# A two-pass filter and mixture-of-experts kernel: vector work of the setup put into waits, the first tiles worked off in the setup, and transposes three tiles ahead in the second pass

## The chip, the cores and the metric

The kernel runs on one core of one Trainium2 chip. The metric is the time of one execution on the device, in microseconds (us). Inside the core five engines work side by side, each through its own instructions in order: TensorE (PE: matrix multiplications and transposes), VectorE (DVE), ScalarE (ACT), GpSimd (POOL: here mostly indirect gathers and scatters) and SyncE (SP: it only issues transfers). They meet at semaphores.

## The reference, cut to what matters

The input is x of 16 x 1024 tokens with 512 features each. N is the number of tokens, 16384.

```python
xn = layernorm(x)                                  # per token
# branch s: a filter over the features, and a correction by 24 bits
D    = fractal_dimension(xn)                       # one number, from the first 1024 values of xn
x1   = ifft(fft(xn) * wave_filter(D, 512)).real    # a fixed linear map, given D
bits = (x1 @ W_el + b_el > 0)                      # 24 bits a token
c    = golay_correct(bits)                         # 12 syndromes; up to 3 bits are flipped
s    = x1 + c @ W_le + b_le
# branch g: two of eight experts for each token
p        = softmax(xn @ router_w.T)
w, e     = top2(p);  w = w / (sum(w) + 1e-6)
g        = silu(sum over the two of (xn @ expert_weights[e] + p[e]) * w)
out  = x + s * g
```

Whatever route a token takes, it is multiplied by two 512 x 512 expert matrices in float32.

## The kernel before, in words

**Two passes over 128 tiles of 128 tokens.** The first pass (`pass_1`, L1053) reads x in blocks of four tiles. For each tile g it sums the halves of a row and gets its total (`total`, L422, on DVE), sums the squares (`spread`, L447, on ACT), forms sums and differences for the filter (`fold`, L484: two instructions `sd` on DVE, one `mm` on POOL), transposes the four quarters on PE and copies them to SBUF on ACT (`transpose`, L498), multiplies them with the filter's matrices `cs`, `cd`, `cm` on PE and scales the outcome into `yb` on ACT (`filt`, L512). `scale` (L456) turns the sums of squares of a group of eight tiles into 1/deviation, in three steps on ACT and DVE; `level` (L441) writes the means of four tiles on ACT. Every four tiles `store` (L530) writes `yb` to a DRAM buffer `yd`. Behind this, for groups of 8 and of 16 tiles, run the correction of the bits (`code`, L553) and the routing (`route`, L615), which sorts the tokens by pair of experts into `lists` with indirect scatters (L771).

**The setup** (`setup`, L250, after `loads`, `constants` and `more_constants`) comes ahead of the first pass. A chain that no engine can leave computes D: DVE sums pieces of x, PE adds them over partitions (L267), DVE counts (L272 to L278), PE adds again (L279), ACT takes a logarithm (L282), DVE forms an angle, ACT a sine (L296), DVE scales the bases (L307), PE multiplies them (L311, L316), and ACT and PE complete `cs`, `cd`, `cm` (L325 to L352). After that come `total` and `spread` of the first eight tiles. Tile 0 alone is folded and transposed in the setup.

**Order.** The order on each engine is the order in which the program is written (`tc.manual_schedule()`); nothing reorders it. In pass 1, step g of the loop issues `fold(g + 2)`, a few `total` and `spread` for tiles up to `AHEAD_S` = 11 ahead, `transpose(g + 1)`, two operations of `setup_code` (constants for later, on DVE) and `filt(g)`; then come one scatter and one piece each of the waiting lists `now`, `routes` and `aside`. An entry `None` in a list ends the step's share: `push` (L1037) runs operations up to the next `None`.

```python
            while spreads and spreads[0] <= g + AHEAD_S and spreads[0] <= 2 * g + GT + 4:
```

**The second pass** (from L1380) runs over 189 tiles sorted by experts: 101 "whole" tiles (all their tokens have the same pair of experts, so two products), 61 "items" (leftover rows for one expert, one product, stored to `ed`) and 27 "rest" tiles (they gather two results of items). 28 whole tiles come first, then the items, then 5 whole, then the rest tiles with the other whole ones among them. Step n issues gathers for tiles ahead (`fetch_tok`, `fetch_x`, `fetch_y` on POOL), `normalize(n + AHEAD_N)` on DVE, and then `work_on(tile n)`:

```python
            pe = product(k, 0)
            scaled(k.acc, pe, k)
            beside()
            added(k, product(k, 1))
```

`product` (L1224) is four float32 matrix multiplications of 128 x 128 by 128 x 512 (L1228). `beside()` issues `turn(n + AHEAD_T)` (L1191: four transposes into the one buffer `pt2`, L1196, and a copy `xt` by ACT, L1198), `turn_code` (L1245: the corrected bits are transposed on PE, L1249, into a PSUM buffer `pc` with one slot and copied by ACT, L1253) and `mend` (L1255: a product with W_le, L1261). In the opening steps two tiles' `turn_code` and `mend` fall into one step, because the records of tile k are taken to be there at step 1 + k // 2 only (`late`, L1365). While the second pass opens, the last routing still drains through `routes`; at its end `whole_ops(1)` (L842) appends its own steps to `aside`. Their first, `lengths` (L849), multiplies the running counts `cum` on PE (L853); DVE has just updated `cum` (L814).

Of the kernel before, what the change touches and what calls it, by code (L numbers as in the profile page):

```python
# [8 lines left out]
F32 = mybir.dt.float32  # L9
# [8 lines left out]
P = 128  # L18
# [15 lines left out]
def kernel(  # L34
# [154 lines left out]
    def constants():  # L189
# [24 lines left out]
        for i, x_ in enumerate(lx):  # L214
            v.memset(st.slope[:, i : i + 1], -(n * x_ - sum(lx)) / den)
        kf = kf[:, 0:KC]
        kr = sp.tile([P, KC], F32, name="kr")
# [11 lines left out]
        v.tensor_scalar(st.by0[:, 1, :], ka, -1.0, -0.5 * math.pi, ALU.mult, ALU.add)  # L229
        v.memset(eps, EPS)  # L230

    def more_constants():
        v, g = nc.vector, nc.gpsimd

        g.iota(tok, pattern=[[BLK, NB], [1, TPT]], base=0, channel_multiplier=TPT)
        g.iota(ti, pattern=[[0, 1]], base=0, channel_multiplier=1)
        g.iota(qi, pattern=[[P, NITEM]], base=0, channel_multiplier=1)
        g.memset(ioff, 0)
        g.memset(ones_b, 1.0)
        g.memset(cum, 0.0)  # L240
        g.memset(ones_f, 1.0)
        for e in range(NE):
            g.memset(iota_e[:, e : e + 1], float(e))
        for r in recs:
            g.memset(r, 0.0)
            g.memset(bits_of(r)[:, :, L : L + 1], 1.0)
        for py in pys:
            v.memset(py[:, 1, X + H : WY], 0.0)

    def setup():  # L250
# [18 lines left out]
        )  # L269
        nc.tensor.matmul(pm[:, NS - 1 :], st.own, sums[:, NS - 1 :], start=True, stop=True)  # L270
        above = sp.tile([P, NS, HW], F32, name="above")
        v.tensor_tensor(  # L272
# [5 lines left out]
        v.tensor_reduce(cnt, above, AX.X, ALU.add)  # L278
        nc.tensor.matmul(pn, st.all, cnt, start=True, stop=True)  # L279
        ly = sp.tile([P, NS], F32, name="ly")  # L280
        v.tensor_scalar(ly, pn, 1.0, None, ALU.max)
        nc.scalar.activation(ly, ly, AF.Ln)  # L282
        nc.scalar.preload_act_table(AF.Sin)
# [17 lines left out]
        v.tensor_add(wp, lat[:, 0:2, :], lat[:, 2:4, :])  # L301
        v.tensor_sub(wt[:, 2:4, :], lat[:, 0:2, :], lat[:, 2:4, :])
        gain = sp.tile([P, KC], F32, name="gain")
        v.tensor_mul(gain, sn[:, 0, :], sn[:, 1, :])
# [9 lines left out]
        for i in range(2):  # L314
            for c in range(2):
                nc.tensor.matmul(  # L316
                    pys[1][:, i, 0:H], bas[:, 2 + c, i * P : (i + 1) * P], gbas[:, 2 + c, :],
                    start=(c == 0), stop=(c == 1),
                )
        v.tensor_add(wt[:, 0, :], wp[:, 0, :], wp[:, 1, :])  # L320
        v.tensor_sub(wt[:, 1, :], wp[:, 0, :], wp[:, 1, :])
        for g in range(2):
            total(g)
            spread(g)
        nc.scalar.copy(cs[:, X:], pys[0][:, 0, 0:Q])  # L325
        nc.scalar.copy(cd[:, X:], pys[0][:, 1, 0:Q])
        for g in range(2, 4):
            total(g)
            spread(g)
        level()  # L330
        nc.scalar.copy(cm[:, :, X:], pys[1][:, :, 0:H])
        v.tensor_scalar(cs[:, L:X], wt[:, 0, L:], 0.25, None, ALU.mult)
        v.tensor_scalar(cd[:, L:X], wt[:, 1, L:], 0.25, None, ALU.mult)
        v.tensor_scalar(cm[:, :, L:X], wt[:, 2:4, L:], 0.5, None, ALU.mult)
        fold(0)
        transpose(0)
# [5 lines left out]
        for i in range(2):  # L342
            for c in range(2):
# [3 lines left out]
                )  # L347
        for op in scale(0, slice(0, TPT)):
            op()
        nc.scalar.copy(cs[:, 0:L], pw[:, 0, :])  # L350
        nc.scalar.copy(cd[:, 0:L], pw[:, 1, :])
        nc.scalar.copy(cm[:, :, 0:L], pw[:, 2:4, :])  # L352
        for g in range(4, GT):
            total(g)
            spread(g)
        level()

# [55 lines left out]
    def bits_of(rec):  # L413
        return rec.bitcast(BF16)[:, :, BITS : BITS + 32]
# [427 lines left out]
    def whole_ops(part: int):  # L842
# [95 lines left out]

        aside.extend([lengths, None, full, None, rows_, None, where, upto, None, bounded])
        aside.extend([experts, None, fetch, None, None, apart, None, turned, None, kept])  # L940
# [112 lines left out]
    def pass_1():  # L1053
# [11 lines left out]
        rest = setup_code()  # L1065
        scales += scale(0, slice(TPT, GT))
        totals, spreads = list(range(GT, NT)), list(range(GT, NT))
        for g in range(-2, NT):
            if (g + AHEAD_L) % TPT == 0 and 4 <= (g + AHEAD_L) // TPT < NB:
                xts[(g + AHEAD_L) // TPT] = load_block((g + AHEAD_L) // TPT)  # L1070
# [5 lines left out]
            if g % TPT == 1 and g > 1:  # L1076
                take_ex(g // TPT - 1)
            if 0 < g + 2 < NT:
                fold(g + 2)
            level()  # L1080
            steps(scales, 1)
            while totals and totals[0] <= g + AHEAD_S + 1 and totals[0] <= 2 * g + GT + 5:
                total(totals.pop(0))
            while spreads and spreads[0] <= g + AHEAD_S and spreads[0] <= 2 * g + GT + 4:
                spread(spreads[0])
                if spreads.pop(0) % GT == GT - 1:
                    scales += scale((g + AHEAD_S) // GT)
            if 0 < g + 1 < NT:
                transpose(g + 1)
            steps(rest, 2)  # L1090
            if g < 0:
                continue
            filt(g)
# [20 lines left out]

    AHEAD_K, AHEAD_X, AHEAD_P, AHEAD_Y, AHEAD_N, AHEAD_T = 9, 6, 4, 5, 4, 2
    BEHIND = 3
# [7 lines left out]

    room = w2.tile([P, 512], F32, name="room", bufs=1)

    class Tile:
# [63 lines left out]
    def turn(k):  # L1191
        if k.kind == "rest":
            return
        pt = ps_x.tile([P, KC * P], F32, name="pt2")
        for c in range(KC):
            nc.tensor.transpose(pt[:, c * P : (c + 1) * P], k.xn[:, c * P : (c + 1) * P], ident)  # L1196
        k.xt = w1.tile([P, KC, P], F32, name="xt2")
        nc.scalar.copy(k.xt.rearrange("p c t -> p (c t)"), pt)  # L1198
# [46 lines left out]
    def turn_code(k):  # L1245
        if k.kind == "item":
            return
        pc = ps_c.tile([96, P], F32, name="pc")
        nc.tensor.matmul(  # L1249
# [89 lines left out]
    for kind in kinds:  # L1339
        tiles.append(Tile(kind, seen.get(kind, 0)))  # L1340
        seen[kind] = tiles[-1].n + 1
    assert seen == {"whole": NPURE, "item": NITEM, "rest": NREST}
    half = NREST // 2
    now += code(NG - 1)
    routes += route(len(rounds) - 1) + [lambda: whole_ops(1)] + [None] * 5
    for op in (rest_b, rest_c, rest_d, rest_e):
# [13 lines left out]
    def each(n, op):  # L1360
# [4 lines left out]
    late = [1 + k // 2 for k in range(NTILE)]  # L1365
    due = {
        "triple": [max(k - 3, late[k]) for k in range(NTILE)],
        "turn_code": [max(k - 2, late[k]) for k in range(NTILE)],
# [5 lines left out]
    def those(n, name, op):  # L1374
        k = range(max(0, n - 2), min(NTILE, n + 5)) if n >= 0 else ()
        for i in k:
            if due[name][i] == n:
                op(tiles[i])

    with tc.manual_schedule():  # L1380
        gone = 0
        for n in range(-AHEAD_K, NTILE + 2):
# [16 lines left out]
            def beside():  # L1399
                each(n + AHEAD_T, turn)  # L1400
                those(n, "turn_code", turn_code)
                those(n, "mend", mend)
# [131 lines left out]
```

## Time and profile before

| what | value |
|---|---|
| median of 3 runs | 1370.36 us (1369.69 to 1370.8) |
| the profiled execution's own time | 1371.99 us |
| its span, first to last instruction | 1370.0 us |
| PE busy | 1323.9 us (97%) |
| DVE busy | 927.1 us (68%) |
| POOL busy | 884.1 us (65%) |
| ACT busy | 602.7 us (44%) |
| mean granted PE clock | 0.990 |
| largest group: expert products, L1228 | 2104 instructions, 940.0 us busy |

The span is the time between the first and the last instruction of one profiled execution; 1.99 us of its own time lie around it. A busy time counts when an engine executed something, and matrix multiplications overlap, so that a busy PE need not be a PE at its peak. "Idle before" an instruction is put down to whatever released it last. The granted clock is the share of full speed that PE was given; where it is 0.5, an instruction of PE takes twice as long.

### The profile page before, as it was taken

The numbers are of one execution on the slowest core, as the hardware profiler recorded it, in microseconds if no ns is written. First come the engines' busy times: TensorE is split into PE (matmuls) and PEld (weight loads), VectorE is DVE, ScalarE is ACT, GpSimd is POOL, SyncE is SP. The second block draws the span as 40 slices with busy tenths as digits, with TensorE's granted clock in tenths as the row PEclk, the third lists the DMA queues.
The fourth block names the chain that finished last, engine by engine and source line by source line (L and its number), as shares of the span: only waits on it lengthen the run. The fifth ranks groups of instructions, "written<-read, shape, count | busy, mean of one in ns | idle before, by whom it ended". The sixth has DMA issues, their size and how long they took to land.

```text
span 1370.0 us, 18162 instructions
## 1 busy us (share of the span) xinstructions
PE 1323.9 (97%) x4944; PEld 737.5 (54%) x4944; DVE 927.1 (68%) x2635; ACT 602.7 (44%) x1298; POOL 884.1 (65%) x879
## 2 busy tenths in 40 slices
PE   5999999989999999999999999999999999999996
PEld 4887777765444444444444444444444444444442
DVE  6898999974765788611111137787778877787775
ACT  6998999975322222222222223333333333333332
POOL 3367777876767554577554046777777777777741
PEclk9999999999999999999999999999999999999998
DMA  6998877836333432355446244555555555655531
GB/s 216 353 319 283 254 243 238 256 108 201 85 104 107 141 109 76 112 170 168 138 141 190 75 134 136 181 173 179 174 172 183 179 176 175 187 173 175 181 121 39
DMA packets 119216, 233.75 MB, mean 171 GB/s; under 512 B 37356, under 2 KB 71020, under 8 KB 115023
## 3 DMA queue, kind: packets, MB, share of 16 engines
q0 software_dynamic: 47264, 135.54, 32.8%
q1 hardware_dynamic: 71386, 96.88, 21.2%
q8 instruction: 43, 0.70, 0.2%
q14 instruction: 55, 0.44, 0.1%
q10 hardware_dynamic: 468, 0.19, 0.1%
HBM read 144.79 MB, written 87.75 MB: 170 GB/s over the span
## 4 chain that ended last, share of the span: by engine, by line
PE 82%; DVE 7%; issue 4%; ACT 2%; POOL 2%; DMA 1%; POOLq 0%; DVEq 0%; SPq 0%; ACTq 0%
PE pe L1228 62%; PE py L521 5%; PE pt L1196 5%; PE pt L502 3%; PE py L518 2%; PE py L519 2%; PE pg L1261 1%; DVE pp L431 1%; DVE sd L490 1%; POOL out L1312 1%; DMA yd<-yb 1%; ACT no L451 1%; DVE sd L493 1%; ACT yb L524 1%; PE pc L1249 1%
## 5 line engine op out<-in xcount | busy, mean ns | idle before, releaser
L1228 PE MATMUL pe<-w_sb,xt 128*128 x2104 | 940.0, 594 | 1.2 <-issue 1.2
L1228 PEld LDWEIGHTS pe<-w_sb,xt 128*128 128x128 f32 x2104 | 394.9, 190 | 417.3 <-issue 411.6
L1279 ACT ACTIVATE acc<-acc,yg 128x512 f32<-128x512 f32 x128 | 92.4, 722 | 406.8 <-DVE acc L1278 406.8
L1278 DVE SCALAR_TENSOR_TENSOR acc<-pe,yg,acc 128x512 f32<-128x512 f32 x101 | 75.7, 749 | 180.2 <-PE pe L1228 180.0
L1198 ACT COPY xt<-pt 128x512 f32<-128x512 f32 x162 | 93.6, 578 | 171.7 <-PE pt L1196 171.7
L1312 POOL DMA_INDIRECT out<-xg,toks x101 | 112.3, 1112 | 82.0 <-DVE xg L1307 55.5
L771 POOL DMA_INDIRECT lists<-rec,dst x128 | 136.6, 1067 | 33.9 <-issue 22.4
L495 POOL TENSOR_TENSOR mm<-xt 128x256 f32<-128x256 f32 x128 | 101.5, 793 | 82.4 <-PE pt L502 63.5
L1189 DVE TENSOR_SCALAR xn<-xg,entry 128x512 f32<-128x512 f32 x61 | 34.8, 571 | 173.4 <-PE pt L1196 170.1
L521 PE MATMUL py<-cm,pmt 128*128 128x288 f32 x512 | 147.2, 411 | 0.0
L1135 POOL DMA_INDIRECT yg<-yd,toks x101 | 107.2, 1061 | 61.6 <-ACT acc L1279 29.6
L1135 POOL DMA_INDIRECT xg<-in_x,toks x101 | 108.6, 1075 | 40.7 <-issue 27.5
L1275 ACT ACTIVATE acc<-pe,yg 128x512 f32<-128x512 f32 x101 | 68.9, 682 | 135.0 <-PE pe L1228 102.4
L1196 PEld LDWEIGHTS pt<-ident,xn 128*128 128x128 f32 x648 | 81.0, 141 | 86.6 <-issue 84.3
L524 ACT ACTIVATE yb<-py,rec 128x640 f32<-128x640 f32 x128 | 101.5, 793 | 26.8 <-PE py L521 23.0
L1135 POOL DMA_INDIRECT xg<-in_x,entry x88 | 89.9, 1021 | 29.6 <-issue 25.9
L1135 POOL DMA_INDIRECT part<-ed,adr_r x54 | 65.7, 1217 | 65.0 <-DMA ed<-res 48.8
L521 PEld LDWEIGHTS py<-cm,pmt 128*128 128x128 f32 x512 | 91.9, 193 | 13.9
L1196 PE MATMUL pt<-ident,xn 128*128 128x128 f32 x648 | 97.3, 273 | 1.6 <-DVE xn L1189 0.8
L1307 DVE TENSOR_TENSOR xg<-mix,xg 128x512 f32<-128x512 f32 x128 | 88.5, 692 | 4.4
L451 ACT ACTIVATE no<-xt,sum 128x512 bf16<-128x512 f32 x128 | 91.0, 711 | 1.2 <-DVE pp L431 1.2
L1135 POOL DMA_INDIRECT entry<-lists,adr_i x61 | 62.9, 1032 | 41.7 <-DVE xn L1189 24.7
(270 smaller groups left out, 1766.1 us busy)
## 6 DMA issues: line engine op xcount, KB each, us to landing
xt<-in_x SPq DMA_DIRECT2D x32, 1024.0 KB
yd<-yb SPq DMA_DIRECT2D x32, 576.0 KB
yd<-yb SPq DMA_DIRECT2D x32, 512.0 KB
ed<-res SPq DMA_DIRECT2D x61, 256.0 KB
w_sb<-in_expert_w SPq DMA_DIRECT2D x8, 1024.0 KB
yd<-rec SPq DMA_DIRECT2D x36, 64.0 KB
lists<-rec,dst POOLq DMA_INDIRECT x128
xg<-in_x,toks POOLq DMA_INDIRECT x101
```

The lines of the kernel that those rows point to most:

```text
L451: nc.scalar.activation(no, xts[g // TPT][:, g % TPT, :], AF.Square, bias=k.sum[:, j : j + 1], scale=-float(E), accum_out=k.sq2[:, j : j + 1],)
L495: nc.gpsimd.tensor_tensor(m, xr[:, 0:H], xr[:, H:E], ALU.subtract)
L521: nc.tensor.matmul(py[:, 1, 0 : X + H], pmt[:, 2 + c, :], cm[:, c, :], start=(c == 0), stop=(c == 1))
L524: nc.scalar.activation(y_room(g), py[:, :, 0:WY], AF.Copy, scale=k.rec[:, j, 11:12])
L771: dma = nc.gpsimd.indirect_dma_start(out=lists, out_offset=bass.IndirectOffsetOnAxis(ap=st.dst[:, j : j + 1], axis=0), in_=st.rec.bitcast( ...
L1135: nc.gpsimd.indirect_dma_start(out=dst, out_offset=None, in_=src, in_offset=bass.IndirectOffsetOnAxis(ap=idx, axis=0), bounds_check=limit - 1,
L1196: nc.tensor.transpose(pt[:, c * P : (c + 1) * P], k.xn[:, c * P : (c + 1) * P], ident)
L1198: nc.scalar.copy(k.xt.rearrange("p c t -> p (c t)"), pt)
L1228: nc.tensor.matmul(pe.unsqueeze(1), k.xt[:, c, :], w_sb[:, bass.ds(e, 1), c, :], start=(c == 0), stop=(c == KC - 1),)
L1279: nc.scalar.activation(k.acc, k.acc, AF.Silu, bias=k.rec[:, 9:10])
L1307: nc.vector.tensor_add(k.x, k.mix, k.x)
L1312: dma = nc.gpsimd.indirect_dma_start(out=of, out_offset=bass.IndirectOffsetOnAxis(ap=k.tok, axis=0), in_=k.x, in_offset=None, bounds_check ...
```

## The change

The change does the following.

- **Setup.** Eight small DVE operations that prepare the angles (`arguments`) move from `constants` to behind the first sums, where DVE has to wait for PE. The clears of the four record buffers move from POOL to DVE (`clear`): one behind the second count, one behind `total(4)`, two into step 4 of the loop. The clears of the two `py` buffers move behind L281. `total(0)` moves ahead of the scaling of the bases. `spread`, `level` and `fold(0)` are spread among the copies of the setup; `fold(1)` and `transpose(1)` are done in the setup; the second half of group 0 is finished in the loop. Totals and spreads run two a step until they are 11 tiles ahead. The steps g = -2 and -1 issue loads only, so that `setup_code` starts two steps later.
- **`whole_ops`.** Its list starts with one more `None`, and six instead of five stand behind the last routing.
- **Second pass.** Addresses, x and the normalized tile are made one step earlier (10, 7, 5 instead of 9, 6, 4), and transposes three tiles ahead instead of two; tiles 0 to 5 keep their two. Step 3 so turns two tiles. `turn` of an item uses the two `pg` buffers when no routing is left. `pc` becomes four slots of one PSUM tile.

```diff
+        v.memset(eps, EPS)
+        st.kf = kf[:, 0:KC]
+
+    def arguments():
+        v, kf = nc.vector, st.kf
         kr = sp.tile([P, KC], F32, name="kr")
...
-        for r in recs:
-            g.memset(r, 0.0)
-            g.memset(bits_of(r)[:, :, L : L + 1], 1.0)
-        for py in pys:
-            v.memset(py[:, 1, X + H : WY], 0.0)
+
+    def clear(r):
+        nc.vector.memset(r, 0.0)
+        nc.vector.memset(bits_of(r)[:, :, L : L + 1], 1.0)
...
         nc.tensor.matmul(pm[:, NS - 1 :], st.own, sums[:, NS - 1 :], start=True, stop=True)
+        arguments()
...
         nc.tensor.matmul(pn, st.all, cnt, start=True, stop=True)
+        clear(recs[0])
         ly = sp.tile([P, NS], F32, name="ly")
         v.tensor_scalar(ly, pn, 1.0, None, ALU.max)
+        for py in pys:
+            v.memset(py[:, 1, X + H : WY], 0.0)
...
         v.tensor_sub(wt[:, 2:4, :], lat[:, 0:2, :], lat[:, 2:4, :])
+        total(0)
...
+        for g in range(1, 4):
+            total(g)
         v.tensor_add(wt[:, 0, :], wp[:, 0, :], wp[:, 1, :])
         v.tensor_sub(wt[:, 1, :], wp[:, 0, :], wp[:, 1, :])
-        for g in range(2):
-            total(g)
-            spread(g)
+        spread(0)
+        level()
+        fold(0)
+        spread(1)
         nc.scalar.copy(cs[:, X:], pys[0][:, 0, 0:Q])
         nc.scalar.copy(cd[:, X:], pys[0][:, 1, 0:Q])
-        for g in range(2, 4):
-            total(g)
-            spread(g)
-        level()
-        nc.scalar.copy(cm[:, :, X:], pys[1][:, :, 0:H])
...
-        fold(0)
+        spread(2)
+        nc.scalar.copy(cm[:, :, X:], pys[1][:, :, 0:H])
         transpose(0)
...
-        for op in scale(0, slice(0, TPT)):
-            op()
+        spread(3)
+        fold(1)
+        begin, middle, end = scale(0, slice(0, TPT))
+        begin()
         nc.scalar.copy(cs[:, 0:L], pw[:, 0, :])
         nc.scalar.copy(cd[:, 0:L], pw[:, 1, :])
         nc.scalar.copy(cm[:, :, 0:L], pw[:, 2:4, :])
-        for g in range(4, GT):
-            total(g)
-            spread(g)
-        level()
+        middle()
+        transpose(1)
+        end()
+        total(4)
+        spread(4)
+        clear(recs[1])
+        total(5)
+        spread(5)
...
-        aside.extend([lengths, None, full, None, rows_, None, where, upto, None, bounded])
+        aside.extend([None, lengths, None, full, None, rows_, None, where, upto, None, bounded])
...
-        scales += scale(0, slice(TPT, GT))
-        totals, spreads = list(range(GT, NT)), list(range(GT, NT))
+        totals, spreads = list(range(6, NT)), list(range(6, NT))
         for g in range(-2, NT):
+            if g == 4:
+                clear(recs[2])
+                clear(recs[3])
...
-            if 0 < g + 2 < NT:
+            if g < 0:
+                continue
+            if g + 2 < NT:
                 fold(g + 2)
...
-            while totals and totals[0] <= g + AHEAD_S + 1 and totals[0] <= 2 * g + GT + 5:
+            while totals and totals[0] <= g + AHEAD_S + 1 and totals[0] <= 2 * g + GT:
                 total(totals.pop(0))
-            while spreads and spreads[0] <= g + AHEAD_S and spreads[0] <= 2 * g + GT + 4:
+            while spreads and spreads[0] <= g + AHEAD_S and spreads[0] <= 2 * g + GT - 1:
...
-    AHEAD_K, AHEAD_X, AHEAD_P, AHEAD_Y, AHEAD_N, AHEAD_T = 9, 6, 4, 5, 4, 2
+    AHEAD_K, AHEAD_X, AHEAD_P, AHEAD_Y, AHEAD_N, AHEAD_T = 10, 7, 4, 5, 5, 3
...
+    pcs = ps_c.tile([96, 4, P], F32, name="pc")
...
-        pt = ps_x.tile([P, KC * P], F32, name="pt2")
+        if k.kind == "item" and not (routes or aside):
+
+            pt = ps_g.tile([P, KC * P], F32, name="pg")
+        else:
+            pt = ps_x.tile([P, KC * P], F32, name="pt2")
...
-        pc = ps_c.tile([96, P], F32, name="pc")
+        pc = pcs[:, k.at % 4, :]
...
-    routes += route(len(rounds) - 1) + [lambda: whole_ops(1)] + [None] * 5
+    routes += route(len(rounds) - 1) + [lambda: whole_ops(1)] + [None] * 6
...
     due = {
+        "turn": [max(k - AHEAD_T, min(k - 2, 3)) for k in range(NTILE)],
...
-                each(n + AHEAD_T, turn)
+                those(n, "turn", turn)
```

## The prediction

> **What bounds the kernel now.** I read four views in this order: the busy times by stretch, what PE waited for, the order of time at the places where it waited, and the granted clock there. The first, with columns start:end, length, busy us of PE, weight loads, DVE, ACT and POOL (with counts), granted clock, DMA share, GB/s:
>
> ```profile
> 0.00:25.00 25.00, 9.51 (x39) 7.97 (x40) 14.94 (x87) 15.06 (x43) 7.04 (x37) 0.91 0.70 255
> 25.00:50.00 25.00, 25.00 (x144) 20.72 (x143) 23.46 (x78) 24.23 (x59) 10.58 (x12) 0.95 0.71 246
> 50.00:75.00 25.00, 24.98 (x166) 20.10 (x166) 21.22 (x80) 24.76 (x63) 8.47 (x12) 1.00 1.01 364
> 75.00:100.00 25.00, 24.99 (x161) 20.26 (x162) 23.21 (x86) 23.78 (x56) 16.01 (x19) 1.00 0.98 306
> ...
> 470.00:800.00 330.00, 330.00 (x1004) 161.93 (x1003) 121.46 (x266) 90.70 (x171) 165.10 (x160) 1.00 0.41 127
> 800.00:1340.00 540.00, 540.00 (x1604) 262.81 (x1603) 418.01 (x1030) 179.41 (x360) 401.61 (x360) 1.00 0.55 170
> ```
>
> From 470 to 1340 us PE has no gap at full clock: a transpose three tiles ahead has nothing to win there. Time can come only from the setup, from pass 1, where ACT is as full as PE, and from PE's few waits (us in total, times, longest):
>
> ```profile
> PE pt L502 <- DVE sd L490: 8.2, 7, 5.2
> PE py L267 <- DVE sums L265: 6.3, 1, 6.3
> ...
> PE pg L853 <- DVE cum L814: 2.6, 1, 2.6
> ...
> PE pc L1249 <- ACT ct L1253: 2.2, 3, 1.0
> ```
>
> The wait of 5.2 us lies ahead of tile 1's transposes, at 23.83. The early loop on ACT, in order of time (start, duration):
>
> ```profile
> 30.36 0.71 ACT L451 ACTIVATE no<-xt,sum 128x512 bf16<-128x512 f32 x1
> ...
> 31.06 0.58 ACT L504 COPY pmt<-pt 128x512 f32<-128x512 f32 x1
> 31.62 0.79 ACT L524 ACTIVATE yb<-py,rec 128x640 f32<-128x640 f32 x1
> 32.31 0.71 ACT L451 ACTIVATE no<-xt,sum 128x512 bf16<-128x512 f32 x1
> ```
>
> One tile is 0.70 + 0.56 + 0.69 = 1.95 us of ACT by starts, with no gap, and PE's tiles are 1.95 us apart too. So a tile started earlier is worth only what ACT's own queue gets ahead.
>
> **Setup: 2.0 us won (0.5 to 4).** Before, DVE reaches L263 at 5.81, though `head` is needed there only and its last packet ended at 2.2. Behind L209 (3.11) stand eight angle operations up to 5.71; they take 0.38 to 0.62 each, and those of their kind at 1.5 to 1.8 took 0.17. They run beside POOL's clears of the records (3.27 to 5.96). With both gone, L263 starts near 3.7, 2.1 earlier. The eight operations now stand behind L265, some 1.3 us unstretched, where DVE waited 1.1 for PE: 0.2 late. The clear of a record (0.51 + 0.17 on POOL, taken for DVE) fits the next wait of 0.68; those of `py`, 0.12, fit the 0.27 behind L281. `total(0)`, 0.42, now waits for block 0 (POOL started on it at 8.35, released by that transfer) and the scaling of the bases waits behind it, another 0.25. With the chain 2.1 - 0.2 = 1.9 early, ACT's last table load ends near 10.4, not 12.2, and the first spread starts there instead of at 12.75: ACT is 2.4 ahead.
>
> From there I count ACT to the start of tile 4's `yb` (35.62 before); the spreads done by then, 0 to 15, are the same 16. ACT's idle time before was 0.69 + 0.48 + 0.19 + 0.74 and some 0.2 of small gaps: 2.3. After: 0.5 until totals 1 to 3 are there (`level` now stands second), 1.1 at the copy of `cm` (PE's L316 runs 3.62 at its cold rate and ends near 14.5), 0.45 ahead of `pmt`, and 0.5 because `total(4)` stands behind `end()` on DVE, which waits for ACT's square, and behind it `total(5)` with a clear between: 2.55. `level` of the second half adds 0.2. 2.4 - 0.25 - 0.2 = 1.95. So `yb` of tile 0 comes near 21.8 instead of 27.7, 6 us earlier, but that of tile 4 only 2 us. The later steps hold the same instructions; the two clears in step 4 (about 1.2 on DVE) and `setup_code` two steps later are covered by ACT, which paces steps 0 to 4 at 2.8 to 3.1 us and the later ones at 1.95 or more. If that cover fails, above all in steps 9 and 10 where L549 and the bits come to DVE too, they cost about 1. The transfers on SP keep their order and move with the tiles.
>
> **The wait for `cum`: 4.1 us won (2.57 to 4.4).**
>
> ```profile
> 381.71 3.60 PE L1228 MATMUL pe<-w_sb,xt 128*128 x8
> ...
> 387.64 0.19 DVE L814 TENSOR_TENSOR cum<-cum,mo 128x28 bf16<-128x28 bf16 x1
> ...
> 387.88 0.23 PE L853 MATMUL pg<-ones_b,cum 128*28 128x128 bf16 x1 [2.57 <-DVE cum L814]
> 388.04 5.40 PE L1228 MATMUL pe<-w_sb,xt 128*128 x8
> ```
>
> L853 stands behind step 5's last product; `cum` is behind `added` of the same step and four routing operations on DVE. One `None` puts L853 behind step 6, by which time `cum` is 5 us old: 2.57 saved. The next product took 5.40 instead of 3.60, and the clock says why:
>
> ```profile
> 385.67:389.09 3.42, 1.21 (x4) 0.67 (x5) 3.35 (x10) 0.72 (x1) 1.69 (x2) 1.00 0.10 15
> 389.09:392.50 3.41, 3.41 (x6) 1.35 (x5) 2.56 (x7) 0.00 (x0) 2.80 (x3) 0.50 0.45 154
> ```
>
> After 3.4 us with 1.21 busy, PE got half its clock for 3.4 us. [...] In this trace windows with 2.46 of 3.4 busy kept the clock and those with 1.64 or less lost it; taking 1.5 idle as the border, a gap of 2.57 at a random phase crosses it in (3.41 + 2.57 - 3.0) / 3.41 = 87%: 2.57 + 0.87 x 1.80 = 4.1. What is late next: step 6's second product needs the buffer that DVE's L1266 and L1267 free (ended 389.1) and would start at 389.5, so 0.4 is left. In pass 1 the same L853 did not wait; its later steps come one later, and `fetch` comes at the same step, for it waits for 16 scatters.
>
> **Turning two tiles in step 3: 2.2 us lost (1.2 to 3.0).**
>
> ```profile
> 363.75 0.58 ACT L1198 COPY xt<-pt 128x512 f32<-128x512 f32 x1
> 364.22 0.27 ACT L1253 CAST ct<-pc 96x128 bf16<-96x128 f32 x1
> 364.54 0.22 PE L1249 MATMUL pc<-ident_b,b 128*96 128x128 bf16 x1 [0.96 <-ACT ct L1253]
> ```
>
> Here tile 6 is turned in the same step as tile 5, with one `pt2`. Its transposes wait for tile 5's copy (to 364.4), end at 364.8; its own copy goes ahead of `ct` on ACT (0.58), so `ct` ends at 365.8, the second `pc` and L1261 follow, and the product, at 364.81 before, starts at 366.1: 1.3. Behind the waiting transposes stand both `pc`, L1261 and tile 3's second product. PE is idle about 1.9 in 2.5 us; by the same border that costs half a clock window in some 52% of phases, 0.9 on average. The four slots of `pc` save nothing: the second L1249 of the changed program is built with a wait for the same count of ACT as before, all four being parts of one PSUM tile. A gain is excluded: nothing is removed there.
>
> **Everything else of the second pass: 0 (-0.5 to +0.5).** The gathers are the same in number, one step earlier; POOL's first `yg` waits 5.2 us for the last store, which covers one gather of 1.0. Item tiles use two buffers where PE never waited for one. Rests of 1.2 to 6 us at POOL and DVE cover `normalize` one step earlier.
>
> **Sum.** 2.0 + 4.1 - 2.2 = 3.9 us. It is made on the profiled execution, 1371.99 us (span 1370.0 and 1.99 around it), which lies 1.63 above the median; a difference carries over: 1370.36 - 3.9 = **1366.5 us**. The bounds of the parts, taken as independent (squares added: 2.0, 0.3, 1.0 and 0.5 upward, 1.5, 1.5, 0.8 and 0.5 downward), give 2.3 to each side: 1364.2 to 1368.8 for this case.
>
> **Rivals.** (1) *The early tiles keep their lead* (8%): if PE and not ACT set the pace of steps 0 to 4, all 6 us stay: 6 + 4.1 - 2.2 = 7.9, 1362.5. For it speaks PE's clock of 0.95 in 25 to 50; against it ACT's 24.23 of 25.
>
> (2) *The setup is swallowed* (18%). From 50 to 100 DMA is busy at 1.01 and 0.98. If its backlog and not the tiles sets the stall that ends with an 11.71 us store at 108.9, nothing of the 2.0 arrives, or half-rate windows in the ramp, where PE has only 1.95 us of work in 3, eat it: 4.1 - 2.2 = 1.9, 1368.5. Against it: DMA is at 0.29 from 24 to 36, so the backlog begins with the tiles.
>
> (3) *The wait moves on* (7%): step 6 then waits for DVE where 0.4 us is left; 2.5 of the 4.1 go: 1.4 won, 1369.0.
>
> (4) *Slower* (7%): ACT's `yb` of tile 36, behind that store, is 2.8 us late today. Were earlier loads to queue ahead of it, a landing of 16 us instead of 11.7 would lose the 3.9; from there on the kernel is slower, at 20 us about 1374. The unchanged order on SP speaks against it.
>
> **How the numbers follow.** The likeliest case has 60%, its own range 1364.2 to 1368.8. A measurement tells 0.2%, 2.7 us, from no change: faster is below 1367.6. Of the 60, 47 lie there and 13 within; rival 1 adds 8 to faster; rival 2 gives 5 to faster and 13 to the same; rival 3 gives 7 to the same; rival 4 gives 7 to slower: 60, 33, 7. The range leaves out rival 4, half of rival 1 and a little of each end: 1361.8 to 1369.6.
>
> **What would show it.** L263 near 3.7 and L267's wait near 4.2, the first `yb` near 22, tile 4's near 33.6, the end of pass 1 (last L521, 326.2 before) 2 us earlier; no wait at the multiplication of `cum` and full clock behind it; a wait of about 1 us at the second transposes of step 3 and no fewer waits at `pc`; from 470 on the same spacing of products. Wrong would make it a stall of another length at tiles 36 to 39, or a half-clock window where I have none.

## The result, and the profile after

The changed kernel took 1363.84 us (median of five runs, 1362.22 to 1366.36), the kernel before beside it 1370.36: a ratio of 0.9955 (95% interval 0.9943 to 0.9966), 6.5 us faster where I had forecast 3.9. The median lies just below the 1364.2 to 1368.8 of the likeliest case and inside the whole range. On the chip of a later comparison it was 1364.16 against 1372.37, 0.9947 (0.9932 to 0.9963). The profiled execution is the one of 1366.36 us, span 1364.3, so the traces show 5.7 us (1370.0 - 1364.3).

The busy times by stretch of the changed kernel, in the columns of the first view shown before:

```profile
0.00:25.00 25.00, 13.38 (x62) 10.87 (x62) 18.19 (x100) 16.41 (x44) 7.28 (x32) 1.00 0.83 297
25.00:50.00 25.00, 24.56 (x135) 19.73 (x136) 22.06 (x77) 24.84 (x63) 8.06 (x10) 0.93 0.70 248
50.00:75.00 25.00, 24.98 (x165) 19.99 (x164) 22.25 (x86) 24.78 (x62) 8.62 (x11) 1.00 0.98 326
...
470.00:800.00 330.00, 330.00 (x1004) 161.90 (x1003) 118.87 (x260) 90.50 (x172) 169.60 (x164) 1.00 0.42 129
800.00:1340.00 540.00, 540.00 (x1597) 262.33 (x1596) 422.64 (x1042) 180.50 (x361) 389.17 (x359) 1.00 0.56 169
```

PE has 13.38 us of work in the first 25, where it had 9.51; from 25 on ACT is full as before (24.84 of 25), and from 470 on nothing has changed. What PE waited for (us in total, times, longest):

```profile
PE py L530 <- ACT pmt L516: 5.5, 3, 3.0
PE py L269 <- DVE kr L222: 3.9, 1, 3.9
...
PE pt L514 <- DVE sd L502: 2.6, 4, 1.0
...
PE pt L1216 <- ACT xt L1218: 1.7, 2, 0.9
...
PE pc L1269 <- ACT ct L1273: 1.3, 2, 0.9
```

The wait of 5.2 for `sd` and the one for `cum` are gone, the first sums are waited for 3.9 instead of 6.3 (the row names `kr`, which ends 0.08 us behind the sums), and a second wait of 0.9 for `xt` is new. The wait for `pmt`, a copy of ScalarE in the first tiles, has grown from 2.4 to 5.5. The setup on ScalarE, the first spread and `yb` of tiles 0 and 4, in order of time (start, duration), before:

```profile
12.75 0.72 ACT L451 ACTIVATE no<-xt,sum 128x512 bf16<-128x512 f32 x1 [0.52 <-DVE pp L431]
...
27.71 0.79 ACT L524 ACTIVATE yb<-py,rec 128x640 f32<-128x640 f32 x1 [0.74 <-PE py L521]
...
35.62 0.80 ACT L524 ACTIVATE yb<-py,rec 128x640 f32<-128x640 f32 x1
```

and in the changed kernel, with ScalarE's longest rest on the way to them:

```profile
9.48 0.72 ACT L463 ACTIVATE no<-xt,sum 128x512 bf16<-128x512 f32 x1
...
11.73 0.21 ACT L456 ACTIVATE low<-sum 128x4 f32<-128x4 f32 x1 [1.44 <-DVE pp L443]
...
21.96 0.77 ACT L536 ACTIVATE yb<-py,rec 128x640 f32<-128x640 f32 x1
...
33.31 0.80 ACT L536 ACTIVATE yb<-py,rec 128x640 f32<-128x640 f32 x1
```

Forecast for the spread and the two `yb` were 10.4, 21.8 and 33.6. And the two places of the second pass, PE in order of time; first step 3 with its two turns, then `cum`:

```profile
360.61 0.60 PE L1216 MATMUL pt<-ident,xn 128*128 128x128 f32 x4
362.07 0.66 PE L1216 MATMUL pt<-ident,xn 128*128 128x128 f32 x4 [0.87 <-ACT xt L1218]
362.57 0.22 PE L1269 MATMUL pc<-ident_b,b 128*96 128x128 bf16 x1
363.56 0.22 PE L1269 MATMUL pc<-ident_b,b 128*96 128x128 bf16 x1 [0.78 <-DVE mix L1292]
...
363.84 3.60 PE L1248 MATMUL pe<-w_sb,xt 128*128 x8
...
387.61 0.60 PE L1216 MATMUL pt<-ident,xn 128*128 128x128 f32 x4
...
391.85 0.23 PE L865 MATMUL pg<-ones_b,cum 128*28 128x128 bf16 x1
392.00 3.70 PE L1248 MATMUL pe<-w_sb,xt 128*128 x8
```

No wait stands ahead of L865, and the product behind it runs at full rate (3.70 where it was 5.40). The row of the second `pc` names `mix` of DVE, which ends at 363.52. The copy `ct`, which that row named before, ends at 363.51, and I read the wait as one for `ct`.

Where the 5.7 us come from, by how much earlier the same instruction starts: the first product of the second pass 3.63 us (326.74 for 330.37); the second `pc` of step 2 only 2.31 (352.42 for 354.73); step 3's product 0.97 (363.84 for 364.81); the transposes of step 6 5.66 (387.61 for 393.27), of which 0.15 goes back when L865 comes. So pass 1 gave 3.6, the first steps of the second pass lost 1.3, the double turn lost 1.3, `cum` gave 4.5: 5.5 of 5.7. The loss of 1.3 was in no step of the prediction.

### The profile page after: what moved, and what is told of

It reads as the page before. It is cut to its first block, busy times and chain, and to the rows that moved or that the text cites. A ratio compares the mean times of both kernels' runs of the same rounds, so it can differ in the third digit from the quotient of the medians.

```text
span 1364.3 us, 18153 instructions
## 1 busy us (share of the span) xinstructions
PE 1324.6 (97%) x4944; PEld 737.2 (54%) x4944; DVE 927.4 (68%) x2643; ACT 602.8 (44%) x1298; POOL 869.5 (64%) x871
## 4 chain that ended last, share of the span: by engine, by line
PE 85%; DVE 4%; issue 4%; ACT 2%; DMA 2%; POOL 1%; POOLq 0%; SPq 0%; DVEq 0%; ACTq 0%
PE pe L1248 62%; PE py L533 7%; PE pt L514 3%; PE pt L1216 3%; PE py L530 2%; PE py L531 2%; PE pg L1216 2%; PE pg L1281 1%; DMA yd<-yb 1%; ACT no L463 1%; POOL out L1332 1%; ACT yb L536 1%; PE pg L581 1%; PE pc L1269 1%; DMA xt<-in_x 0%
## 5 line engine op out<-in xcount | busy, mean ns | idle before, releaser
L533 PE MATMUL py<-cm,pmt 128*128 128x288 f32 x512 | 147.9, 412 | 0.0
L536 ACT ACTIVATE yb<-py,rec 128x640 f32<-128x640 f32 x128 | 101.6, 794 | 25.0 <-PE py L533 20.3
L1151 POOL DMA_INDIRECT part<-ed,adr_r x54 | 62.8, 1164 | 64.9 <-DMA ed<-res 48.7
L1218 ACT COPY xt<-pg 128x512 f32<-128x512 f32 x55 | 32.2, 586 | 153.9 <-PE pg L1216 153.9
L533 PEld LDWEIGHTS py<-cm,pmt 128*128 128x128 f32 x512 | 91.9, 193 | 13.9
L1326 DVE TENSOR_TENSOR mix<-mix,acc 128x512 f32<-128x512 f32 x128 | 87.6, 685 | 0.8 <-ACT acc L1299 0.8
L1216 PEld LDWEIGHTS pt<-ident,xn 128*128 128x128 f32 x428 | 53.4, 141 | 58.4 <-issue 52.2
```

Source lines behind the costliest of these rows:

```text
L533: nc.tensor.matmul(py[:, 1, 0 : X + H], pmt[:, 2 + c, :], cm[:, c, :], start=(c == 0), stop=(c == 1))
L536: nc.scalar.activation(y_room(g), py[:, :, 0:WY], AF.Copy, scale=k.rec[:, j, 11:12])
L1151: nc.gpsimd.indirect_dma_start(out=dst, out_offset=None, in_=src, in_offset=bass.IndirectOffsetOnAxis(ap=idx, axis=0), bounds_check=limit - 1,
L1326: nc.vector.tensor_mul(k.mix, k.mix, k.acc)
```

## The experiments

The kernel before took 1372 us in the runs of front_only, two_buffers, warm_entry and after_again; that chip and the one of the result are called the quiet ones here. It took 1447 and 1460 us in the two other groups. On those chips every kernel stands still for long in the second pass (the one before by its time, the others in their traces), as in this wait of PE in the page of no_ahead:

```profile
PE pc L1264 <- ACT ct L1268: 23.9, 3, 21.6
```

The copy that PE waits for there stands on ScalarE behind rests that the profile puts down to nothing it shows. Pass 1 runs as on the quiet chips up to tile 120. Its last seven tiles already take 17.1 to 17.8 us there, not 14.6, and from the last group of pass 1 to the first product of the second pass it is 7.2 to 8.3 us, not 5.0 to 5.3. The steps between the stalls have their usual lengths again. So from those groups I read positions up to tile 120 and durations; their ratios have wide intervals and decide nothing about a few us.

**cum_only, cum_only_2: the step of `cum` alone.**

```
-        aside.extend([lengths, None, full, None, rows_, None, where, upto, None, bounded])
+        aside.extend([None, lengths, None, full, None, rows_, None, where, upto, None, bounded])
-    routes += route(len(rounds) - 1) + [lambda: whole_ops(1)] + [None] * 5
+    routes += route(len(rounds) - 1) + [lambda: whole_ops(1)] + [None] * 6
```

> The kernel before with one step more ahead of the counting matmul of `cum`, and nothing else. The prediction's row says 2.57 us of wait and 1.80 us of half clock behind it go, weighed 4.1: some 1366.3 us, no gap ahead of that matmul, the granted clock 1.00 behind it. [...] A third reading comes from the trace of the changed kernel, whose pass 1 gains another 1.3 us between tiles 112 and 120, where the same edit shifts the first part's counting by a step: then 5.5 us go, 1364.9, and pass 1 of this kernel ends 1.3 us earlier than before.

> The same kernel as cum_only, on another chip, since the first one stalled some tens of us in the second pass. By the traces so far 2.73 us of idle and counting and 1.80 us of half clock go and 0.16 of the counting comes back a step later: 4.4 us, a ratio to the kernel before of 0.9968. If only the wait counts (2.57): 0.9981. The end of pass 1 is that of the kernel before, within the 1.7 us of one half-clock window.

Measured 0.9927 (0.989 to 0.9965) and 0.9933 (0.9908 to 0.9958), both among stalls. PE has no wait at the counting in either trace, and the product behind it takes 3.70. Pass 1 gains nothing: `yb` of tile 120 starts at 311.62 and 311.91, before 311.67. The reading that counts a gain in pass 1 is refuted. Both intervals lie below the 0.9968 of the row: some 10 us went where 4.4 were expected. A step more may move the stalls too; that was not tested, and these ratios don't size the term. On the quiet chips the edit was not run alone, but from step 3's product to the end of the span it is 1005.2 us in both traces with the wait (before, front_only) and 1000.5 to 1000.9 in the four without it: 4.3 to 4.8.

**setup_only, setup_only_2: the setup alone**, the second pass and `cum` as before.

> The kernel before with the setup and the first steps of the changed one, its second pass and the step of `cum` unchanged. The prediction says 2.0 us are won (0.5 to 4): 1368.4 us, with `yb` of tile 4 and of tile 112 both some 2 us early. If the 3.6 us by which pass 1 of the changed kernel ended earlier in its trace all belong to the setup, 1366.8. If the early lead is swallowed before the end of pass 1, 1370.4.

> The same kernel as setup_only, on another chip. By the prediction 2.0 us, a ratio of 0.9985. By the positions in the traces since (2.7 us at tile 8, another 0.75 between tiles 40 and 104) 3.4 us, 0.9975. The constants alone were measured at 0.9985 (0.9977 to 0.9994); if the new order of the first tiles adds nothing, this run agrees with that.

Measured 0.9985 (0.9951 to 1.002) and 0.9985 (0.9961 to 1.0008): undecided. In the traces `yb` of tile 4 starts at 32.23 and 33.05 (35.62 before) and that of tile 120 at 308.17 and 307.39 (311.67 before): the 3.6 us by which pass 1 of the changed kernel ends earlier come with the setup alone. Both still hold the wait for `cum`, in other executions and on other chips. PE in setup_only:

```profile
405.64 3.60 PE L1243 MATMUL pe<-w_sb,xt 128*128 x8
411.80 0.23 PE L865 MATMUL pg<-ones_b,cum 128*28 128x128 bf16 x1 [2.56 <-DVE cum L826]
```

and two clock windows of setup_only_2 (the first view's columns; PE busy, and the granted clock after POOL):

```profile
409.80:413.22 3.42, 0.99 (x3) 0.58 (x4) 3.35 (x9) 0.72 (x1) 2.81 (x3) 1.00 0.49 151
413.22:416.63 3.41, 3.41 (x5) 1.35 (x4) 2.74 (x7) 0.00 (x0) 2.50 (x4) 0.50 0.07 18
```

In all four traces that have the wait with PE idle in it (before, setup_only, setup_only_2, front_only) it is 2.56 or 2.57 and the product behind takes 5.40. The half clock follows a window with 0.99 us of 3.42 busy here, 1.21 in the trace of before, and it belongs to the price.

**warm_gap: the wait kept, PE busy in it.**

```
+            if part:
+                for _ in range(5):
+                    nc.tensor.matmul(pg, ident, w_sb[:, 0, 0, :], start=True, stop=True)
             nc.tensor.matmul(k.pc, cum, ones_b, start=True, stop=True)
```

> The kernel before with five more matmuls of 128x512 (about 2.1 us of PE) into the same PSUM tile just ahead of the second part's counting matmul of `cum`, which overwrites them: the wait for `cum` stays as long, but PE is not idle in it. If a window with about a third of busy PE brings half clock, the product behind the wait takes 3.6 us instead of 5.4 and the kernel is 1.8 us faster, 1368.6 us. [...]

```profile
402.54 4.45 PE L856 MATMUL pg<-w_sb,ident 128*128 128x512 f32 x10
406.92 0.23 PE L857 MATMUL pg<-ones_b,cum 128*28 128x128 bf16 x1
407.08 3.70 PE L1232 MATMUL pe<-w_sb,xt 128*128 x8
```

The product behind takes 3.70 and not 5.40: with PE busy in the wait, no half clock followed in this trace. But the five run in ten passes of 0.43, twice what I had counted, and last 4.4 us where the wait plus the lost clock was 4.4: mechanism shown, time none (0.996, 0.9918 to 1.0002).

**front_only: the constants of the setup alone.** The order of totals, spreads, folds and transposes stays.

```
-        for r in recs:
-            g.memset(r, 0.0)
...
+        arguments()
         above = sp.tile([P, NS, HW], F32, name="above")
...
+        clear(recs[0])
         ly = sp.tile([P, NS], F32, name="ly")
```

> The kernel before with only the constants part: the angle arguments behind the first sums, the clears of the records and of `py` on VectorE in its waits; the order of totals, spreads, folds and transposes is untouched. The prediction puts the win of the setup into this front chain (1.9 us early, 2.4 on ScalarE) and counts the new order of tiles as nothing or 0.2 lost: then the first spread starts near 10 us, `yb` of tile 8 comes 2 to 2.7 us before the 43.9 of the kernel before, as in the run with the whole setup (41.4 on average of three), and pass 1 ends as early as there. The rival: the tiles folded and turned in the setup bring it; then `yb` of tile 8 here stays within 1 us of 43.9.

Measured 0.9985 (0.9977 to 0.9994), 1370.45 against 1372.37 us. ScalarE, the first spread and `yb` of tile 8:

```profile
10.85 0.72 ACT L458 ACTIVATE no<-xt,sum 128x512 bf16<-128x512 f32 x1 [1.38 <-DVE pp L438]
...
41.63 0.80 ACT L531 ACTIVATE yb<-py,rec 128x640 f32<-128x640 f32 x1
```

Start of `yb` in the traces, us (old setup: before, cum_only, cum_only_2, warm_gap; new: the nine others without front_only):

| tile | old setup | constants alone | new setup |
|---|---|---|---|
| 0 | 27.1 to 27.8 | 25.42 | 20.8 to 22.4 |
| 8 | 43.3 to 44.9, mean 44.2 | 41.63 | 40.4 to 42.1, mean 41.4 |
| 120 | 310.8 to 311.9, mean 311.5 | 308.26 | 304.6 to 310.2, mean 307.2 |

The first spread starts at 10.85, not near 10: it waits 1.38 for its total. On the means the new order is 3.8 us ahead of the constants alone at tile 0, and at tile 8 some 0.2. Up to there the constants carry the gain, the tiles folded and turned early hardly any, and the rival expectation falls; but the constants alone have one trace, and at tile 8 the nine others differ by 1.7.

Behind tile 8 this does not hold. At tile 120 the new order is 1.1 us ahead, and in the time the constants alone won 1.9 of the 8.2 us of the changed kernel on that chip. With 4.8 for `cum` and 1.3 lost by the double turn, 4.7 of the 8.2 belong to the setup. The start of the second pass took 1.4 from the constants alone in their trace (under warm_entry), which is why 3.4 us at tile 120 (311.67 to 308.26) became 1.9 in the time. By this estimate some 1.4 us are left for the new order. That is not clear of the noise (the 1.9 alone has an interval of 0.8 to 3.2), and how the new order would bring them is open.

**after_again: the changed kernel once more.**

> The changed kernel once more, for comparison on the same chip and for a second reading of step 3 and of the first product: the transposes of tile 6 wait 0.8 to 0.9 us for the single buffer, step 3's product starts 11.4 us behind the second `pc` of step 2 where that of the kernels with two tiles ahead starts 10.1 behind it, and the granted clock behind step 3 is 1.00 or 0.50 by the phase of the 3.41 us windows. The time against the kernel before: 0.9955 as in the result.

The distance from the second `pc` of step 2 to step 3's product is 11.42 us in both traces of the changed kernel (352.42 to 363.84, 347.49 to 358.91) and 10.08 in those with two tiles ahead (354.73 to 364.81; front_only and warm_entry the same): the double turn costs 1.34. A half-clock window followed in neither: the granted clock is 1.00 from 360.04 to 366.87 in the first trace and from 340 to 430 in the second.

**two_buffers: tile 6 turned in a PSUM buffer of its own.**

```
-        if k.kind == "item" and not (routes or aside):
+        if k.at == 7 or k.kind == "item" and not (routes or aside):
```

> The changed kernel with one edit: the transposes of tile 6, the second ones of step 3, get their own PSUM buffer from the pool of the routing products. By the prediction the wait of the second transposes for the copy out of the single buffer (0.86 us in the trace) is gone; the copy of tile 6 still stands ahead of `ct` on ScalarE, so the second `pc` waits longer than 0.77, about 1.2, and step 3's product starts 0.4 to 0.9 us earlier than the 11.4 us behind `pc` of step 2 that the changed kernel shows. If the buffer is not what delays it, that distance stays 11.4. In the whole time 0.4 to 0.9 us less than the changed kernel, too little to tell.

```profile
359.84 0.60 PE L1216 MATMUL pg<-ident,xn 128*128 128x128 f32 x4
360.28 0.22 PE L1269 MATMUL pc<-ident_b,b 128*96 128x128 bf16 x1
361.51 0.22 PE L1269 MATMUL pc<-ident_b,b 128*96 128x128 bf16 x1 [1.01 <-DVE mix L1290]
361.57 0.38 PE L1281 MATMUL pe<-wle,ct 96*128 96x512 bf16 x1
361.79 3.60 PE L1248 MATMUL pe<-w_sb,xt 128*128 x8
```

No wait stands ahead of the second transposes, the second `pc` waits 1.01 (here too `mix` and `ct` end within 0.02 us of each other), and the distance is 10.57: 0.85 of the 1.34 was the single buffer, 0.49 the rest of the second turn, its copy on ScalarE ahead of `ct` among it. The time, 1364.12 us, is the changed kernel's within what can be told.

**no_ahead, no_ahead_2: two tiles ahead as before**, setup and `cum` changed.

> The changed kernel with the second pass's queue of transposes, gathers and PSUM slots put back to two tiles ahead: the setup and the step of `cum` stay changed. The prediction's term for the double turn says this is 2.2 us faster than the changed kernel (1.2 to 3.0): 1361.6 us. The trace of the changed kernel, where the double turn cost about 1.3 us and no half-clock window followed, says 1362.5. If the three-tile lead gains anything later, it is slower than that, 1363.8 or more.

> The same kernel as no_ahead (setup and `cum` changed, two tiles ahead as before), on another chip. If the three parts add up: 3.4 + 4.4 = 7.8 us, 0.9943 of the kernel before, 1.3 us faster than the changed kernel's 0.9947 to 0.9955. In step 3 the product starts 10.1 us behind the second `pc` of step 2, as in the kernels with two tiles ahead. If the three-tile lead pays somewhere later, the ratio is no lower than 0.9950.

Measured 0.9898 (0.9836 to 0.996) and 0.9915 (0.9876 to 0.9954), on the chips with stalls: no verdict on 1.3 us. Clear of stalls, from the first `pc` of step 3 the second follows 1.19 us later and the product 0.27 behind it (389.39, 390.58, 390.85), as before (363.36, 364.54, 364.81).

**warm_entry: two tiles ahead, and PE kept busy at the start of the second pass**, by 6, 6 and 10 transposes of a constant ahead of the first two turns and the first product.

```
+        if k is tiles[0] or k is tiles[1]:
+            warm(6)
         pt = ps_x.tile([P, KC * P], F32, name="pt2")
...
+        if k is tiles[0] and h == 0:
+            warm(10)
         e = expert(k, h)
```

> The changed kernel with two tiles ahead as before, and with idle transposes of a constant (6, 6 and 10, written to a routing buffer and read by nobody) in PE's three waits at the start of the second pass. If the half clock at the start of the second pass comes from PE being less than half busy in a 3.41 us window, the first product takes 3.6 us, not 5.4 to 6.7, and the kernel is 1.8 to 3.1 us faster than with two tiles ahead alone. [...]

```profile
323.74 1.25 PE L1209 MATMUL pg<-ident 128*128 128x128 f32 x10
324.97 3.70 PE L1252 MATMUL pe<-w_sb,xt 128*128 x8
...
338.65 0.26 PE L1273 MATMUL pc<-ident_b,b 128*96 128x128 bf16 x1 [2.24 <-DVE b L1267]
...
340.17 5.29 PE L1252 MATMUL pe<-w_sb,xt 128*128 x8
```

The first product is at full rate, and no gain shows: 1363.61 us, where the changed kernel took 1364.16 with the double turn in it. Two tiles ahead without the fillers was not run on this chip. PE comes earlier to the first `pc`, waits there 2.24 instead of 0.9, and half clock follows: the product at 340.17 takes 5.29. The same happened in front_only without fillers, where no half clock fell on the first product (3.69): the window from 338.83 to 342.24 has 1.22 us busy, and the clock in the next is 0.50. From the start of the last L521/L533 group to the second `pc` of step 2 it is 29.5 to 29.6 us with one half window at the entry (before, after_again, two_buffers; the first product takes 5.38 or 5.39), 30.9 to 31.0 with none there (front_only, warm_entry; 3.69 and 3.70), and 30.9 with two (the profiled changed kernel; 6.67). What holds the first `pc` is a chain off PE; POOL, ScalarE and VectorE in warm_entry:

```profile
329.64 1.01 POOL L1150 DMA_INDIRECT yg<-yd,toks  x1 [5.73 <-DMA yd<-yb]
...
333.30 0.69 ACT L1299 ACTIVATE acc<-pe,yg 128x512 f32<-128x512 f32 x1 [8.77 <-DMA yg<-yd,toks]
...
334.01 0.75 DVE L1302 SCALAR_TENSOR_TENSOR acc<-pe,yg,acc 128x512 f32<-128x512 f32 x1 [8.26 <-ACT acc L1299]
...
338.40 0.30 DVE L1267 COPY b<-yg 128x96 bf16<-128x96 bf16 x2
```

The first gather waits for the last store, `acc` for the gather, and twelve routing operations, a normalization and `acc` lie on VectorE ahead of `b`. From that last group to `b` it is 18.5 to 19.0 us in five traces, whatever PE's clock; only with two half windows (20.3) is PE the later one.

**code_first: the first `pc` ahead of the tile's transposes in steps 2 and 3**, on top of no_ahead.

```
+                for k in first:
+                    turn_code(k)
                 each(n + AHEAD_T, turn)
```

> no_ahead with one edit in steps 2 and 3: the first of the two codes is transposed ahead of the tile's transposes, not behind them, so that its copy `ct` stands ahead of the copy of the tile on ScalarE. The second `pc` waits 0.92 and 0.96 us in the kernel before; here the 0.44 of transposes lie in that wait, and the copy of 0.58 is behind. I expect 0.4 us less in step 2, where the second `ct` is needed in the same step, and 0.8 in step 3: the product of step 3 starts some 1.2 us earlier counted from the second `pc` of step 1 than in no_ahead_2. In the whole time 1 us, less than can be told. If `pc` waits for something else, the distances stay.

```profile
377.56 0.22 PE L1264 MATMUL pc<-ident_b,b 128*96 128x128 bf16 x1
377.62 0.61 PE L1211 MATMUL pt<-ident,xn 128*128 128x128 f32 x4
378.70 0.22 PE L1264 MATMUL pc<-ident_b,b 128*96 128x128 bf16 x1 [0.47 <-ACT ct L1268]
...
378.97 3.60 PE L1243 MATMUL pe<-w_sb,xt 128*128 x8
```

From the first of these to the product it is 1.41 us, in no_ahead_2 from the transposes (388.95) to the product (390.85) 1.90: 0.49 won in step 3, not 0.8. The second `pc` still follows the first by 1.14: `ct` (378.40) now stands behind `acc`, the scaling of the first product on ScalarE (377.81, 0.69 us), and no longer behind the copy of the tile. Step 2 lies in a stall and could not be read. 0.9896 (0.9854 to 0.9938) beside no_ahead_2's 0.9915 on the same chip is no difference. No version was shown faster than the changed kernel.

## Why the prediction was right, and where it was off

**Setup: 2.0 us won.** The mechanism was right, the size low. The cut starts at 3.32 instead of 3.7, the first spread at 9.48 instead of 10.4; `yb` of tile 4 is 2.3 us early where 2.0 was forecast, and the lead of tile 0 (27.71 to 21.96, 5.75) shrinks as forecast, since ACT paces: rival 1 is refuted. Over all traces the lead is 2.8 at tile 8 and 4.3 at tile 120. The mis-sized term is "2.4 ahead" on ScalarE: it was 3.3 (12.75 to 9.48), because its last table load starts 2.75 us earlier (8.19 for 10.94) where 1.9 was counted. Of this ScalarE gave back 1.0 by tile 4, not 0.45: ahead of `level` it rests 1.44 and not 0.5, since totals 1 to 3 stand behind DVE's scaling of the bases, which took 1.43 us where it had taken 1.01. Behind tile 8 the prediction had nothing; the traces gain another 0.7 between tiles 64 and 72, where the trace of before has a wait of 0.42 for `sd` that the changed kernel's has not, and 1.0 between 104 and 120, where a half-clock window lay between 270 and 290 us in four of four traces with the old setup and in four of nine with the new (four products `py` of 128x288 take 1.61 to 2.13 us there, 1.13 otherwise). That the new setup makes such windows rarer was not tested; nine traces can't tell it from luck. Tiles 32 to 40 gave half a microsecond back on the mean. Rival 2, the gain swallowed by the stall at tiles 36 to 39, is refuted: tiles 32 to 40 take 20.4 to 23.2 us with the old setup and 21.0 to 23.4 with the new. The same range holds rival 4 off.

**The wait for `cum`: 4.1 us won.** Right: 4.5 in the trace. The row, wait and half clock together (2.57 + 1.80), gave the size; the wait alone is 2.57. Rival 3 didn't happen: no wait stands in step 6.

**Double turn in step 3: 2.2 us lost.** The 1.3 of waits was right to a tenth, though shared out otherwise. The 0.9 for a half-clock window was wrong, and the step that failed is the border of "1.5 idle". Step 3 of the changed kernel by clock windows:

```profile
360.04:363.45 3.41, 1.88 (x11) 1.12 (x10) 3.27 (x12) 1.85 (x4) 2.59 (x3) 1.00 0.23 73
363.45:366.87 3.42, 3.31 (x10) 1.60 (x9) 1.36 (x3) 0.32 (x2) 2.71 (x3) 1.00 0.27 75
```

1.53 us idle, and the clock stayed. The two waits here are 0.87 and 0.78, 1.65 together where 1.9 was counted. The windows that lost the clock behind the setup in the traces of the two kernels had 1.98 idle or more (3.41 less the 1.43 busy from 322.50 in the changed kernel).

**The slots of `pc` and the rest: 0.** Right: the second `pc` of step 2 waits 0.92 as before, and 0.2 us of the span is left unassigned. From the thirteenth `pc` to the end it is 943.8 to 944.5 us in all six traces of the quiet chips, with two tiles ahead or three.

**What was missing: the start of the second pass.** The profiled execution lost 1.3 us there, which hid part of the gain. By clock windows, before:

```profile
327.65:331.06 3.41, 1.40 (x7) 0.87 (x7) 2.10 (x4) 1.17 (x2) 1.24 (x2) 1.00 0.95 313
331.06:334.47 3.41, 3.41 (x6) 1.36 (x5) 0.00 (x0) 0.00 (x0) 0.09 (x1) 0.50 0.69 252
```

and in the changed kernel:

```profile
322.50:325.91 3.41, 1.43 (x9) 0.84 (x8) 2.47 (x5) 1.71 (x3) 2.50 (x4) 1.00 1.04 314
325.91:329.32 3.41, 2.58 (x3) 1.17 (x4) 1.33 (x3) 0.26 (x1) 1.00 (x1) 0.50 1.04 375
329.32:332.74 3.42, 3.42 (x5) 1.35 (x4) 0.00 (x0) 0.00 (x0) 1.66 (x2) 0.50 0.41 130
```

Before, one half window lay there. Here the window at half clock had 0.8 idle, another half window followed, and PE became later than the chain behind `b`. after_again had one window and did not lose it. So 5.7 in the profiles and 6.5 in the medians differ as executions do: the mean granted clock of the five runs is 0.991 in the one of 1366.36 us and 0.993 to 0.995 in the others, and one half window, 1.7 us of PE's work (5.40 - 3.70 at the product behind `cum`), is 0.00125 of it.

The sum: 3.6 + 4.5 - 1.3 - 1.3 = 5.5 against 2.0 + 4.1 - 2.2 = 3.9. The parts were off by 1.6, 0.4, 0.9 and -1.3, so that the total came as near as it did in part by luck: without the loss at the start of the second pass, which no step of the prediction had, the changed kernel would have been some 6.8 us faster in this execution. Of the setup's 3.6, the mechanism that was forecast brought 2.3 (tile 4); where the rest came from is not shown.

## What to carry to other kernels

A wait of PE cost its length plus the half-clock time behind it at `cum` (2.57 + 1.80), and its length alone at the two waits of step 3 (0.87 and 0.78): read the granted clock behind the wait, and price both. Before keeping PE busy in a gap, ask what the next wait hangs on: here a chain from the last store over a gather and VectorE held the next step, and a faster PE only waited longer at the next `pc` (2.24 for 0.9). A head start of early tiles is worth only what the engine that paces them gains; tile 0 was 5.75 us early, tile 8 only 2.1, or 2.8 on the mean of the traces.

## What the hardware showed unexpectedly

The clock windows of 3.41 us start at another phase in each execution: at 327.65 and 331.06 in the trace of before, at 322.50, 325.91 and 329.32 in that of the changed kernel. Behind the setup, windows at full clock with these busy times of PE were followed by half clock: 0.99 us (setup_only_2, from 409.80), 1.21 and 1.40 (before, 385.67 and 327.65), 1.22 (front_only, 338.83) and 1.43 (the changed kernel, 322.50). These were followed by full clock: 1.42 (setup_only_2, 276.68), 1.62 and 1.79 (front_only, 277.39 and 322.08), 1.71 (no_ahead, 107.61) and 1.88 (the changed kernel, 360.04). So the 1.5 idle that I had used as the border does not part them: 1.53 to 1.99 idle kept the clock, and 1.98 lost it. No run varied the idle time step by step. At half clock, a window with 2.58 busy was followed by another at half clock (the changed kernel, 325.91), one with 2.72 by full clock (before, 283.27). And the kernel before took 1370 to 1372 us on two occasions and 1447 to 1460 on two others. In the traces from those two chips the stalls begin in the last seven tiles of pass 1 and go on in the second pass; their cause is open.
